# Three one-hots to a byte, and a deeper pipeline for the first spreading, in a two-layer graph kernel

## The chip, the cores and the metric

The kernel runs on one core of a Trainium2 chip. The metric is the device time in microseconds, the median of the runs. A separate profiled execution gives the trace that the text reads.

## The reference

There are 32768 nodes with 128 features and 524288 edges `src -> dst`, sorted by `dst`. Two layers follow one another:

- Layer 0 (cut): `agg = segment_sum(x[src], dst)`, then an MLP with batch norm on `(1 + eps) * x + agg`; attention with 8 heads inside blocks of 512 nodes; a second MLP; batch norms; and `x = layernorm(x + layer0(x))`.
- Layer 1 (cut), three times: `x = 0.5 * x + 0.5 * (softmax((x @ Wq.T + bq) @ keys.T) @ values - 0.2 * (x - dinv * scatter_add(dinv * x)))`. This is a memory lookup with 512 keys and a sum over the same edges in the other direction. Two layer norms end it.

So four times in all, rows are sent along the edges and summed at the other end.

## The kernel before, in words

Nodes are cut into 256 windows of 128 (`NW = 256`), or 64 blocks of four windows (`NB = 64`). Rows are kept as three bf16 parts (`ROW = 384` numbers), so that sums are exact enough. An exchange of rows along edges has two halves:

1. **Spreading** (`Exchange.spread`, L1444 to L1457). For each source window, a one-hot matrix of 128 lanes by 1536 slots (`SL = 2 * KS * P`) says which row goes to which slot. TensorE multiplies it with the window's rows, two blocks of 128 slots at a time, into a PSUM tile `exp` (L1449). VectorE or ScalarE turns each `exp` into bf16 in `y_o` (L1454). The two halves of `y_o` are stored into `slots` in HBM by the SP queue (L1457).
2. **Sums** (`Sums`, `Exchange.add`). For each destination window, `y_i` is loaded from `slots` (L1462), some rows are gathered by GpSimd (`listed`, L1471), VectorE makes a one-hot `oh` (L1482), and 19 matmuls per window add into `seg` (L1496).

The one-hot for spreading is called `pick`; it is 1 where a slot's listed lane equals the partition, and it is stored as fp8, in which 1.0 is the byte 0x38. In layer 0 each spreading makes its own `pick`. For layer 1, `keep_pick` (L1434) makes it once per window while layer 0's sums run, and stores it in HBM, 1536 bytes a partition (`pick_d`). The three spreadings of layer 1 load it again (`known_pick`, L1408, L1410), on the SP queue, two windows ahead (`ask_pick`, L2093).

The stages that the change touches, in order of time in the profile:

- `spread_x` (about 2330 to 3570 us): layer 0's spreading. Its order is written out by hand (`manual_schedule`). Window by window it loads x blocks (`load`, L1827), rows of the listing broadcast to all partitions (`row_of`, L1839, for odd windows; even ones use matmuls `row_p`, L1424), makes `pick` on VectorE (L1845, L1849), splits the rows (L1398 to L1400, L1396), and spreads. `sort_on` issues some of the sorting steps that a later stage needs after each pair of matmuls, so their number goes with the windows. `y_o`, `band` and `pick` have two buffers, `xe` three.
- `layer0_grid` (about 3570 to 5310 us): layer 0's sums, with part of the attention woven in; also written by hand. Per window, VectorE has the attention's maxima (L1642), the next window's `oh`, the `pick` for layer 1 (L1439, stored by L1441), and, when the window's sum has ended, its close (L1973, L1975; ScalarE's L1976 then frees the only `seg` buffer).
- the first loop of `layer1_grid` (about 5570 to 6770 us): the first spreading of layer 1, with layer 0's last norms. A scheduler sets the order from priorities (the numbers beside the steps). Every third eviction is VectorE's, the others ScalarE's.
- the second loop (about 6770 to 9010 and 9010 to 11180 us): sums of one step, the memory lookup, and the spreading of the next step, all woven together by the scheduler. Every fourth eviction is VectorE's.

The last stage (from 11180 us) has sums and the lookup only.

Of the kernel before, what the change touches and what calls it, by code (L numbers as in the profile page):

```python
# [9 lines left out]
F32 = mybir.dt.float32  # L10
I32 = mybir.dt.int32
# [9 lines left out]
P = 128  # L21
# [889 lines left out]
def tile_gnn_resnorm(ctx: ExitStack, tc: tile.TileContext, a: dict, out: bass.AP):  # L911
# [413 lines left out]
    rows_d = [dram(f"rows{t}", (N, ROW + 2 * (t == T_STEPS)), BF16) for t in range(T_STEPS + 1)]  # L1325
    pick_d = dram("pick", (NW, P, SL), FP8)
    gc = {}

    def grid_consts(pool):
        gc["iota1"] = pool.tile([P, P], BF16, name="iota1")  # L1330
        nc.vector.tensor_scalar(gc["iota1"], iota, 1.0, None, op0=OP.add)
        gc["lane1"] = pool.tile([P, 1], F32, name="lane1")
        nc.vector.tensor_scalar(gc["lane1"], lane_f, 1.0, None, op0=OP.add)
        gc["down"] = pool.tile([P, P], BF16, name="down")
        nc.vector.tensor_copy(gc["down"], gc["lane1"].to_broadcast([P, P]))
        gc["ident"] = pool.tile([P, P], BF16, name="ident_b")
        nc.vector.tensor_copy(gc["ident"], ident)
# [18 lines left out]
    class Exchange:  # L1356
# [8 lines left out]
        def __init__(self, key, slots, table):  # L1365
            self.grid, self.slots, self.table = grid.out[key], slots, table
            self.width = table.shape[1]
            self.bands = {}

        def load_rows(self, pool):  # L1370
# [37 lines left out]
        def known_pick(self, wp, w):  # L1408
            pick = wp.tile([P, SL], FP8, name="pick", bufs=3)
            nc.sync.dma_start(pick, pick_d[w])  # L1410
            return pick

# [21 lines left out]
        def keep_pick(self, wp, w, count):  # L1434

            def one():
                self.load_band(wp, w + 2)
                pick = wp.tile([P, SL], FP8, name="pick", bufs=2)
                nc.vector.tensor_scalar(pick, self.bands.pop(w), gc["lane1"], None, op0=OP.is_equal, op1=OP.add,  # L1439
                                        accum_out=count, saturate=False)  # L1440
                nc.sync.dma_start(pick_d[w], pick)  # L1441
            return [one]

        def spread(self, wp, pp, tag, w, pick, r, m, st, to_dve):  # L1444

            ps = pp.tile([P, 2, BLK], F32, name="exp", tag=tag)
            for j in range(2):
                o = (2 * m + j) * P
                nc.tensor.matmul(ps[:, j, :ROW], pick[:, o:o + P], r, start=True, stop=True)  # L1449
            if m == 0:  # L1450
                st["y"] = wp.tile([P, 2, KS, ROW], BF16, name="y_o")
            y = st["y"]
            dst = y.rearrange("p h r d -> p (h r) d")[:, 2 * m:2 * m + 2, :]
            (nc.vector.tensor_copy if to_dve else nc.scalar.copy)(dst, ps[:, :, :ROW])  # L1454
# [358 lines left out]
    def spread_x():  # L1813

        ex = Exchange("dst", slots_d[1], rows_d[T_STEPS])
        with tc.tile_pool(name="l0r", bufs=1) as gp, tc.tile_pool(name="l0e", bufs=2) as wp, \
                tc.tile_pool(name="l0e_p", bufs=2, space=PSUM) as p_k, \
                tc.tile_pool(name="l0e_e", bufs=3, space=PSUM) as p_e:
            grid_consts(gp)
            ex.load_rows(gp)  # L1820
            xb, rows, ends, picks, bands, y = {}, {}, {}, {}, {}, {}
            more = {"steps": grid.build_more(lane, Bank(p_k, "row_p")), "quota": 0.0}

            def load(b):
                if b < NB:
                    xb[b] = wp.tile([P, NCH, D], F32, name="xe", bufs=3)
                    nc.sync.dma_start(xb[b], rows_of(a["x"], b))  # L1827
# [6 lines left out]
            def row_of(w):  # L1834

                if w < NW:
                    bands[w] = wp.tile([P, SL], BF16, name="band")
                    src = ex.grid["row"][w % P:w % P + 1, w // P * SL:(w // P + 1) * SL]
                    nc.sync.dma_start(bands[w], src.to_broadcast([P, SL]))  # L1839
# [24 lines left out]
            with tc.manual_schedule():  # L1864
                load(0)
                load(1)
                split(0)
                for f in ends.pop(0):
                    f()
                row_of(1)  # L1870
                for j in range(SL // BLK):
                    pick(0, j)
                for w in range(NW):
                    b, c = divmod(w, NCH)
                    if w % 2:
                        row_of(w + 2)
                    if c == 0:
                        load(b + 2)
                        split(b + 1)
# [134 lines left out]
    def layer1_grid(v_d, s3, c3):  # L2014

        exs = [Exchange("src", slots_d[t % 2], rows_d[t]) for t in range(T_STEPS)]
        with tc.tile_pool(name="l1g", bufs=1) as gp:
            exs[0].load_tables(gp)
            for e in exs[1:]:
                e.slot, e.other, e.shared = exs[0].slot, exs[0].other, exs[0].shared  # L2020
            picked = {}

            def ask_pick(wp, w):
                if w < NW:
                    picked[w] = exs[0].known_pick(wp, w)

# [57 lines left out]
            def emit(t, b, st, wp, p_e, share):  # L2084
# [339 lines left out]
```

## Time and profile before

| | us |
|---|---|
| median of 5 runs (12862.94 to 12888.74) | 12870.88 |
| the profiled execution | 12879.18 |
| its span | 12877.0 |

| in the profiled execution | busy us | share |
|---|---|---|
| TensorE matmuls | 11136.2 | 86% |
| VectorE | 9300.9 | 72% |
| ScalarE | 6899.5 | 54% |
| GpSimd | 6111.3 | 47% |
| DMA, bytes moved | 3672.92 MB | mean 285 GB/s |

A share over the whole span mixes stages with different limits, so it says little by itself; the stages are read one by one below. A line such as "A <- B: 35.9, 42, 3.9" means that A waited for B 35.9 us in total, 42 times, at most 3.9 us. In a group of instructions, "x256" counts them, then follow the busy time, the mean time of one in ns, and the idle time of the engine just before them, with what ended it.

### The profile page before, as it was taken

What the parts mean: (1) busy time and instruction counts of PE and PEld (TensorE: products, weight loads), DVE (VectorE), ACT (ScalarE), POOL (GpSimd) and SP (SyncE); (2) the same over time, 40 slices, a digit from 0 to 9 for tenths busy, and PEclk for the clock granted to TensorE, in tenths of its full rate; (3) what the DMA queues carried; (4) which work ended last, traced back from release to release, by engine and by line L of the source; (5) the groups of instructions that cost most, each with busy time, mean ns of one, the idle gap of its engine ahead of it and who ended that gap; (6) DMA issues with size and microseconds to landing.
All of it is one profiled execution on the core that took longest, in us unless ns stands there. A gap on an engine that the chain in (4) does not pass through costs nothing.

```text
span 12877.0 us, 164812 instructions
## 1 busy us (share of the span) xinstructions
PE 11136.2 (86%) x57832; PEld 5540.5 (43%) x57832; DVE 9300.9 (72%) x14876; ACT 6899.5 (54%) x10523; POOL 6111.3 (47%) x5525
## 2 busy tenths in 40 slices
PE   7798798666679999966668999999999999899998
PEld 2233233332334444433324555555555555455554
DVE  7977977799778888666665666665566666587777
ACT  4455455677722333467775666666566666533333
POOL 0084075000067777200005666665666666577777
PEclk9899899899999999988889999999999999999999
DMA  1000000688899999779999999999999999988887
GB/s 44 10 15 20 10 14 14 239 327 325 325 320 334 334 338 343 262 287 342 345 344 336 400 397 396 393 393 375 377 398 398 395 395 391 361 293 290 287 289 254
DMA packets 1401340, 3672.92 MB, mean 285 GB/s; under 512 B 218802, under 2 KB 633682, under 8 KB 1399346
## 3 DMA queue, kind: packets, MB, share of 16 engines
q1 hardware_dynamic: 960496, 2952.44, 61.1%
q0 software_dynamic: 252608, 520.41, 12.5%
q10 hardware_dynamic: 187394, 189.42, 4.4%
q8 instruction: 457, 7.49, 0.2%
q14 instruction: 385, 3.15, 0.1%
HBM read 2175.76 MB, written 1485.80 MB: 284 GB/s over the span
## 4 chain that ended last, share of the span: by engine, by line
PE 43%; DMA 19%; DVE 18%; POOL 8%; ACT 7%; issue 4%; ACTq 0%; SPq 0%; DVEq 0%; POOLq 0%
PE seg L1496 14%; DMA slots<-y_o 12%; PE exp L1449 10%; ACT y_o L1454 5%; DVE y_o L1454 3%; PE s L2120 3%; POOL listed L1471 3%; PE s L1658 3%; DMA listed<-rows,other 3%; DVE mx L1642 3%; PE pv L1669 2%; PE tr L2126 2%; PE s L2132 1%; POOL moved L661 1%; POOL mask L662 1%
## 5 line engine op out<-in xcount | busy, mean ns | idle before, releaser
L1471 POOL DMA_INDIRECT listed<-rows,other x5120 | 5099.0, 996 | 4049.2 <-issue 2919.7
L1454 ACT CAST y_o<-exp 128x768 bf16<-128x768 f32 x4480 | 3380.4, 805 | 1229.7 <-PE exp L1449 759.3
L1449 PE MATMUL exp<-rows,pick 128*128 128x384 bf16 x10752 | 2558.6, 346 | 758.4 <-ACT y_o L1454 363.2
L1496 PEld LDWEIGHTS <-oh 128*128 128x128 bf16 x19456 | 1900.8, 98 | 1893.5 <-issue 803.6
L1496 PE MATMUL seg<-y_i,oh 128*128 128x384 bf16 x12288 | 2430.0, 327 | 17.9 <-DMA y_i<-slots 16.5
L1454 DVE CAST y_o<-exp 128x768 bf16<-128x768 f32 x1664 | 1587.3, 954 | 994.8 <-PE exp L1449 780.7
L1449 PEld LDWEIGHTS <-pick 128*128 128x128 fp8e4 x10752 | 1089.6, 102 | 2077.3 <-issue 1386.1
L1662 ACT ACTIVATE pT<-s 128x1024 f32<-128x1024 f32 x1024 | 1048.8, 1025 | 1174.9 <-PE s L1637 829.9
L1642 DVE TENSOR_REDUCE mx<-s 128x2 f32<-128x1024 f32 x1024 | 1246.0, 1220 | 283.0 <-PE s L1637 270.2
L1496 PE MATMUL seg<-listed,oh 128*128 128x384 bf16 (+1 forms) x5120 | 1208.2, 329 | 241.1 <-DMA listed<-rows,other 176.2
L1658 PE MATMUL s<-ql,k 32*128 32x512 f32 x4096 | 1225.1, 676 | 158.8 <-DVE mx L1642 146.2
L1637 PE MATMUL s<-k,q 32*128 32x512 f32 x4096 | 1232.7, 683 | 15.8 <-ACT pT L1662 10.8
L2196 DVE SCALAR_TENSOR_TENSOR part<-seg,dinv,part 128x128 f32<-128x128 f32 x1536 | 531.4, 346 | 946.7 <-PE seg L1496 935.0
L2120 PE MATMUL s<-keysT,qT 128*128 128x512 f32 x1536 | 812.5, 611 | 3.0 <-ACT pr L1064 1.8
L1482 DVE TENSOR_TENSOR oh<-iota,slot 128x2432 bf16<-128x2432 bf16 x512 | 725.0, 1416 | 4.2 <-DMA slots<-y_o 3.0
L1482 DVE TENSOR_TENSOR oh<-ramp_p,slot 128x2432 bf16<-128x2432 bf16 x512 | 722.3, 1411 | 3.4 <-DMA slots<-y_o 3.3
L1064 ACT ACTIVATE pr<-s,nm 128x512 f32<-128x512 f32 x768 | 533.4, 695 | 325.3 <-DVE nm L1062 324.0
L2132 PE MATMUL s<-pt,values 128*128 128x512 f32 x1536 | 699.5, 595 | 2.7 <-ACT pt L2127 2.7
L1658 PEld LDWEIGHTS s<-ql,k 32*128 32x128 f32 x4096 | 323.7, 193 | 691.2 <-DVE mx L1642 298.8
L1062 DVE TENSOR_REDUCE nm<-s 128x1 f32<-128x512 f32 x768 | 515.0, 681 | 121.9 <-PE s L2120 121.3
L1393 POOL MEMSET rows<- 128x8 bf16 x64 | 6.7, 106 | 1250.8 <-PE exp L1449 710.0
L1496 PE MATMUL seg<-common,oh 128*128 128x384 bf16 (+1 forms) x2048 | 586.8, 330 | 5.1 <-DMA common<-rows,shared 4.9
(409 smaller groups left out, 13930.6 us busy)
## 6 DMA issues: line engine op xcount, KB each, us to landing
slots<-y_o SPq DMA_DIRECT2D x2048, 576.0 KB
y_i<-slots SPq DMA_DIRECT2D x1024, 1152.0 KB
pick<-pick SPq DMA_DIRECT2D x1024, 192.0 KB
listed<-rows,other POOLq DMA_INDIRECT x5120
rows<-rows SPq DMA_DIRECT2D x192, 384.0 KB
band<-row_dst SPq DMA_DIRECT2D x128, 384.0 KB
band<-row_src ACTq DMA_DIRECT2D x256, 192.0 KB
x_d<-xn SPq DMA_DIRECT2D x128, 256.0 KB
```

What stands on the lines that cost most here:

```text
L1064: nc.scalar.activation(pr, s, AF.Exp, bias=nm, accum_out=sums)
L1449: nc.tensor.matmul(ps[:, j, :ROW], pick[:, o:o + P], r, start=True, stop=True)
L1454: (nc.vector.tensor_copy if to_dve else nc.scalar.copy)(dst, ps[:, :, :ROW])
L1471: nc.gpsimd.indirect_dma_start(out=g[:, k, :], out_offset=None, in_=self.table, in_offset=bass.IndirectOffsetOnAxis(ap=index[:, k:k + 1], ...
L1482: nc.vector.tensor_tensor(oh.rearrange("p c (w z) -> p c w z", z=2), ramp.rearrange("p (w z) -> p w z", z=2)[:, None].to_broadcast([P, NC2 ...
L1496: nc.tensor.matmul(ps[:, :n], oh[:, j, :], src, start=(k == 0), stop=(k == NC2 - 1))
L1637: nc.tensor.matmul(ps[:, s % 2, :], t["q", o][32 * s:32 * s + 32, c * P:(c + 1) * P], t["k", o][32 * s:32 * s + 32, :], start=True, stop=True)
L1642: nc.vector.tensor_reduce(m[:, c, 2 * i:2 * i + 2, xr[o]], st[b].pop(("two", i)), AX.X, OP.max, negate=True)
L1658: nc.tensor.matmul(ps[:, s % 2, :], t["k", o][32 * s:32 * s + 32, c * P:(c + 1) * P], t["ql", o][32 * s:32 * s + 32, :], start=True, stop= ...
L1662: nc.scalar.activation(t["p", c][:, 2 * i:2 * i + 2, :], ps, AF.Exp)
L2120: nc.tensor.matmul(s, st["q"][:, c * P:(c + 1) * P], keysT, start=True, stop=True)
L2132: nc.tensor.matmul(ps, values[:, k, :], st["pt"][:, k, :], start=(k == 0), stop=(k == NCH - 1))
```

## The change

There are two parts.

First, the `pick` kept for layer 1 is packed. Its 1536 bytes a partition are seen as 128x384 int32, in three thirds. A byte is 0x38 or 0, that is, bits 3, 4 and 5 are set together. `keep_pick` keeps bit 3 of the first third, bit 4 of the second and bit 5 of the last, in one 128x128 int32 tile (`three`), with one VectorE operation for the last third and one for each of the others, and stores that. A load is then 512 bytes a partition. `unpacked` makes the three thirds again with one VectorE operation (bitwise and with a mask by thirds). A set byte is then 0x08, 0x10 or 0x20, which in fp8 is 1/64, 1/32 or 1/8; the evictions multiply by 64, 32 or 8 (`WEIGHTS`), VectorE's with `tensor_scalar`, ScalarE's with `mul`. The load is asked two windows ahead as before, and unpacked one window ahead, after the third pair of matmuls of a window.

Second, in `spread_x`, `y_o` has five buffers (two elsewhere), `xe` four, `band` three; x blocks are loaded three blocks ahead, bands four windows ahead.

```diff
-    pick_d = dram("pick", (NW, P, SL), FP8)
+    pick_d = dram("pick", (NW, P, P), I32)
+    BITS = (3, 4, 5)
+    WEIGHTS = (64.0, 32.0, 8.0)
...
+        gc["bits"] = some[:, 1:].bitcast(I32)
+        for k in range(3):
+            nc.vector.memset(gc["bits"][:, k:k + 1].bitcast(U8), 1 << BITS[k])
...
         def known_pick(self, wp, w):
-            pick = wp.tile([P, SL], FP8, name="pick", bufs=3)
-            nc.sync.dma_start(pick, pick_d[w])
-            return pick
+            packed = wp.tile([P, P], I32, name="three", bufs=3)
+            nc.sync.dma_start(packed, pick_d[w])
+            return packed
+
+        def unpacked(self, wp, packed):
+            pick = wp.tile([P, 3, P], I32, name="pick")
+            nc.vector.tensor_tensor(pick, packed[:, None, :].to_broadcast([P, 3, P]),
+                                    gc["bits"].unsqueeze(2).to_broadcast([P, 3, P]), OP.bitwise_and)
+            return pick.rearrange("p k n -> p (k n)").bitcast(FP8)
...
                 nc.vector.tensor_scalar(pick, self.bands.pop(w), gc["lane1"], None, op0=OP.is_equal, op1=OP.add,
                                         accum_out=count, saturate=False)
-                nc.sync.dma_start(pick_d[w], pick)
+                packed = wp.tile([P, P], I32, name="three")
+                thirds = pick.bitcast(I32).rearrange("p (k n) -> p k n", k=3)
+                nc.vector.tensor_scalar(packed, thirds[:, 2], 0x01010101 << BITS[2], None, op0=OP.bitwise_and)
+                for k in (1, 0):
+                    nc.vector.scalar_tensor_tensor(packed, thirds[:, k], 0x01010101 << BITS[k], packed,
+                                                   op0=OP.bitwise_and, op1=OP.bitwise_or)
+                nc.sync.dma_start(pick_d[w], packed)
...
-                st["y"] = wp.tile([P, 2, KS, ROW], BF16, name="y_o")
+                st["y"] = wp.tile([P, 2, KS, ROW], BF16, name="y_o", bufs=self.kept)
...
-            (nc.vector.tensor_copy if to_dve else nc.scalar.copy)(dst, ps[:, :, :ROW])
+            if weight is None:
+                (nc.vector.tensor_copy if to_dve else nc.scalar.copy)(dst, ps[:, :, :ROW])
+            elif to_dve:
+                nc.vector.tensor_scalar(dst, ps[:, :, :ROW], weight, None, op0=OP.mult)
+            else:
+                nc.scalar.mul(dst, ps[:, :, :ROW], weight)
...
+            ex.kept = 5
...
-                    xb[b] = wp.tile([P, NCH, D], F32, name="xe", bufs=3)
+                    xb[b] = wp.tile([P, NCH, D], F32, name="xe", bufs=4)
...
-                    bands[w] = wp.tile([P, SL], BF16, name="band")
+                    bands[w] = wp.tile([P, SL], BF16, name="band", bufs=3)
...
-                        row_of(w + 2)
+                        row_of(w + 4)
                     if c == 0:
-                        load(b + 2)
+                        load(b + 3)
                         split(b + 1)
...
                     if m == 0:
                         ask_pick(wp, i + 2)
-                    ex.spread(wp, p_e, "exp", i, picked[i], st["r"][:, c, :], m, y, n % share == share - 1)
+                        if i not in picked:
+                            unpack(wp, i)
+                    ex.spread(wp, p_e, "exp", i, picked[i], st["r"][:, c, :], m, y, n % share == share - 1,
+                              WEIGHTS[m // 2])
+                    if m == 2:
+                        unpack(wp, i + 1)
```

More of the change, by code (lines that the diff above doesn't have):

```diff
@@ L1331, in grid_consts @@
         nc.vector.tensor_scalar(gc["iota1"], iota, 1.0, None, op0=OP.add)
-        gc["lane1"] = pool.tile([P, 1], F32, name="lane1")
+        some = pool.tile([P, 4], F32, name="lane1")
+        gc["lane1"] = some[:, 0:1]
         nc.vector.tensor_scalar(gc["lane1"], lane_f, 1.0, None, op0=OP.add)
@@ L1368, in __init__ @@
             self.bands = {}
+            self.kept = 2
         def load_rows(self, pool):
@@ L1440, in one, with spread @@
                                         accum_out=count, saturate=False)
-                nc.sync.dma_start(pick_d[w], pick)
+                packed = wp.tile([P, P], I32, name="three")
[5 more added lines that the diff above has]
+                nc.sync.dma_start(pick_d[w], packed)
             return [one]
-        def spread(self, wp, pp, tag, w, pick, r, m, st, to_dve):
+        def spread(self, wp, pp, tag, w, pick, r, m, st, to_dve, weight=None):
             ps = pp.tile([P, 2, BLK], F32, name="exp", tag=tag)
@@ L1864, in spread_x @@
             with tc.manual_schedule():
-                load(0)
-                load(1)
+                for b in range(3):
+                    load(b)
                 split(0)
@@ L1870, in spread_x @@
                 row_of(1)
+                row_of(3)
                 for j in range(SL // BLK):
@@ L2020, in layer1_grid, with unpack @@
                 e.slot, e.other, e.shared = exs[0].slot, exs[0].other, exs[0].shared
-            picked = {}
+            asked, picked = {}, {}
             def ask_pick(wp, w):
                 if w < NW:
-                    picked[w] = exs[0].known_pick(wp, w)
+                    asked[w] = exs[0].known_pick(wp, w)
+            def unpack(wp, w):
+                if w in asked:
+                    picked[w] = exs[0].unpacked(wp, asked.pop(w))
             def first(b, st, wp, p_tr, group):
```

## The prediction

> **What bounds the kernel now.** I began with the page's 40 slices, which show several regimes, and then asked for a table by stage. Columns: stage, its length, busy time of TensorE, its weight loads, VectorE, ScalarE and GpSimd, then granted clock, DMA share, GB/s.
>
> ```profile
> core 0: us, PE busy (x) PEld busy (x) DVE busy (x) ACT busy (x) POOL busy (x), PEclk, DMA share, GB/s
> ...
> 2330.00:3570.00 1240.00, 824.17 (x3716) 373.30 (x3716) 1083.98 (x1481) 927.02 (x1318) 12.43 (x70) 0.94 0.88 321
> 3570.00:5310.00 1740.00, 1606.21 (x9263) 787.16 (x9263) 1450.27 (x2046) 499.57 (x861) 1240.35 (x1312) 0.97 0.97 332
> ...
> 5570.00:6770.00 1200.00, 768.38 (x3174) 353.50 (x3175) 772.97 (x1524) 845.37 (x1176) 0.00 (x0) 0.83 0.94 341
> 6770.00:9010.00 2240.00, 2114.87 (x10825) 1178.62 (x10825) 1339.30 (x2153) 1399.20 (x2314) 1369.20 (x1324) 0.99 1.01 385
> 9010.00:11180.00 2170.00, 2056.11 (x10579) 1143.94 (x10577) 1303.82 (x2102) 1351.52 (x2225) 1345.25 (x1301) 1.00 1.02 390
> ```
>
> I call these five S (first spreading), L0 (first layer's sums), P (first spreading of layer 1), W1 and W2 (sums and spreading together). The change touches no other stage. W1 and W2 have a full DMA system (share above 1) and TensorE at 94%. In L0 TensorE, VectorE (83%) and DMA are all near full. P is slack on each engine by itself, so there the handovers bind. S has VectorE at 87%.
>
> Next come the waits inside stages. In S, then in P (who waits for whom, total us, times, longest):
>
> ```profile
> ACT y_o L1454 <- DMA slots<-y_o: 123.6, 105, 3.9
> ...
> DVE pick_b L1845 <- DMA band<-row_dst: 35.9, 42, 3.9
> ```
> ```profile
> DVE y_o L1454 <- PE exp L1449: 322.2, 337, 1.5
> ...
> PE exp L1449 <- DVE y_o L1454: 256.9, 244, 2.4
> ```
>
> In steady L0 (4500 to 5100 us, 91 windows of 6.59 us each) the largest VectorE wait is the one below: it waits for a window's sum to end.
>
> ```profile
> DVE hn L1973 <- PE seg L1496: 39.3, 48, 3.7
> ```
>
> In steady W2 (9300 to 11100 us, 217 one-hots L1482, so 8.29 us a window) TensorE's waits before the spreading are short:
>
> ```profile
> L1449 PE MATMUL exp<-rows,pick 128*128 128x384 bf16 x2595 | 596.8, 324 | 56.0 <-ACT y_o L1454 46.4 <-DVE y_o L1454 1.4 <-DMA pick<-pick 0.7
> ```
>
> **Prices.** VectorE's integer and small groups in the first stage, then three groups of the page (busy, mean ns of one, idle before):
>
> ```profile
> L743 DVE TENSOR_TENSOR moved<-moved,mask 128x768 int32<-128x768 int32 x2 | 1.9, 958 | 0.1
> ...
> L728 DVE TENSOR_SCALAR moved<-moved 128x768 int32<-128x768 int32 x2 | 1.1, 552 | 0.0
> L510 DVE SCALAR_TENSOR_TENSOR sh_a<-keys,word 128x128 f32<-128x128 f32 x2 | 0.6, 292 | 0.1
> ...
> L705 DVE COPY keys<-word 128x128 f32<-128x128 f32 x2 | 0.4, 216 | 0.0
> ```
> ```profile
> L1454 ACT CAST y_o<-exp 128x768 bf16<-128x768 f32 x4480 | 3380.4, 805 | 1229.7 <-PE exp L1449 759.3
> ...
> L1662 ACT ACTIVATE pT<-s 128x1024 f32<-128x1024 f32 x1024 | 1048.8, 1025 | 1174.9 <-PE s L1637 829.9
> ```
>
> - *Unpack*, 128x384 int32, two tensors: L743's 768 take 958 ns and L221's 1024 take 1217, so 1.01 ns an element and 181 fixed: 570 ns by that line, 552 if 128 elements are taken off L2077 (128x512, also with a broadcast operand, 682 ns). I take 0.55 us; 256 in P, W1 and W2 each: 141 us of VectorE a pass.
> - *Pack*, three on 128x128 int32: 216 (L705, one source) + 2 x 285 (just under L510) = 0.79 us a window, 202 us in L0.
> - *ScalarE's scaled eviction* becomes an ACTIVATE: L1662 less 256 elements at 0.86 ns (from L2108's 512 at 584 ns to L1454's 768 at 805) is 804 ns, so nothing. With a pointer operand it would cost 0.1 us more (L2114, 688 for 512, against L2108), 106 us in 1024 a pass; the instruction list names none, so I take 0.
> - *VectorE's scaled eviction*: between 954 (the CAST) and 1012 (L1849's 745 for 512, which has a pointer, plus 256 elements). 0 to 25 us a pass; I take 10.
> - *Loads and stores*: the one-hot goes from 128 packets of 1536 B to 128 of 512 B. The DMA queues between 1500 and 2300 us (almost only 512 B packets on q10), then between 9100 and 11100 us (packets, MB, share of 16 engines):
>
> ```profile
> q10 hardware_dynamic: 8448, 4.20, 1.8%
> ```
> ```profile
> q1 hardware_dynamic: 186094, 652.25, 83.2%
> ```
>
> The first is 1.8% x 800 us x 16 / 8448 = 27 ns for 497 B; the second 143 ns for 3505 B. The line through both gives 67 ns for 1536 B and 28 ns for 512 B. With 8 packets an engine, one load falls from 0.54 to 0.22 us: 0.32 us a window, 81 us of full DMA time in each of L0, P, W1, W2.
>
> A rule speaks against this: the Trainium skill's "DMA: Bandwidth & Descriptors", section Bandwidth, measures 0.95 us for 64 KB and says transfers below that size are descriptor-dominated. By that figure, an estimate, the small load costs 0.73 us more than my row says, and with 0.54 us before it the 81 us saved would become 105 us lost a pass. [...]
>
> **Part by part.**
>
> *S.* Five y_o buffers in place of two, band and x loads further ahead. This removes ScalarE's 124 us of waits for stores and VectorE's 36 for bands (and 13 for stores), but what is late next? From 2400 to 3200 us VectorE is busy 47.2 of each 50 us, because sorting steps are paced by windows and go along with them; that part can shrink by 5.6%, 45 us, and I take 25. From 3200 to 3560 the waits for stores and bands are 34 and 19 us and VectorE has room; I take 25 of the 53. The queue order changes little: the loads move ahead on SP, whose waits there are for evictions. S: -50, between -110 (most of the waits) and +10 (a deeper queue at share 0.88 lengthens each transfer).
>
> *L0.* VectorE's busy time a window is 519.9/91 = 5.71 us, with 0.88 idle. Pack makes it 6.50 of 6.59. Queued behind it are the close of the sum (L1973, L1975), for which ScalarE's L1976 and then TensorE wait (one seg buffer). The 0.43 us a window of waiting for seg can be absorbed; the other 0.45 (uT, bands, aval, handovers) cannot be counted on: 6.50 + 0.45 = 6.95, +0.36 x 256 = +92. The relieved queue gives back part of the stage's waits for bands (39 us on VectorE) and gathered rows (29 us on TensorE): -25. On SP the pick store L1441 now waits for pack, and the y_i load behind it leaves 0.8 us later, covered by its two windows' lead. L0: +67, between -30 (TensorE had all the slack) and +200.
>
> *P.* 141 us more on a VectorE with 427 us idle. The unpack stands between evictions; TensorE already waits 257 us for VectorE's evictions. In the instruction order two of four unpacks of a block fall between plain evictions, where VectorE idles about 1 us each time, and two beside the split or the moments, where they add up. I take a quarter: +35, and 3 for scaled evictions. P: +38, between -20 (the DMA share of 0.94 falls) and +141.
>
> *W1, W2.* The DMA floor falls from 8.29 to 7.97 us a window. TensorE is busy 96% of steady time, 7.97 us too. So both allow at most 81 us a pass; TensorE's waits for y_o and y_i (56 + 5 us in 1800, 75 in 2200) should fall and not vanish. VectorE rises from 61 to 68%, and its evictions are what TensorE hardly waits for (1.4 us). I take 57 a pass, -115 for both; between -162 and +30 (no relief, and a tenth of 282 us of unpacking exposed).
>
> Sum: -50 + 67 + 38 - 115 = -60. The profiled execution took 12879.2 us (span 12877.0), 8 above the median of the five runs, 12870.9. On the median: **12811**.
>
> **Rivals.** *A, slower: VectorE's new work is exposed.* Place: pack before the close in L0, unpack before the evictions in P. Full price 202 + 141 = 343 us, against 190 us of relief (50 + 25 + 115): +153, 13024. It decides from 55% exposed; I have 38% (130 of 343). For: VectorE at 99% in L0 leaves no play, and the profile has 257 us of TensorE behind VectorE in P. Against: half of L0's windows end with VectorE waiting.
> *B, nothing: TensorE holds W1 and W2.* Its 96% is all it needs and half the gain is left, -57: total about -2, 12869. For: the full TensorE. Against: its busy time is modelled, with matmuls in isolated pairs (0.49 us) that would close up.
> *C, faster: DMA time is the limit wherever the share is near 1.* W1 and W2 give 162, S 85, L0 all its 81 against the 92, P nothing: -162 - 85 + 11 = -236, 12635. For: shares of 0.97 to 1.02. Against: L0's VectorE.
> That the one-hot is not smaller in HBM can't be: the stored tensor is 128x128 int32.
>
> **How the numbers follow.** Forecast 0.47, A 0.23, B 0.15, C 0.15. About 0.2% (26 us) is what this kernel's measurement can tell from no change. Faster: forecast 0.44, C 0.15, B 0.03: 0.62. Same: forecast 0.03, B 0.10: 0.13. Slower: A 0.23, B 0.02: 0.25. The range 12680 to 12965 leaves out the far half of A and of C; the forecast's own is 12740 to 12850.
>
> **What would show it.** Right: W1 and W2 near 8.05 us a window with DMA still above 0.97; L0 near 6.85 us with VectorE above 93%; waits of y_o for slots gone from S; the unpack near 550 ns, the three packing operations near 0.79 us together. Wrong: W1 or W2 no shorter (B); L0 over 1900 us or TensorE's wait for VectorE's y_o in P above 350 us (A); the 512 B loads' packets over 50 ns (then the relief is under a half).

## The result, and the profile after

The changed kernel takes **12873.93 us** (median of 25 runs, 12851.41 to 12902.96) beside 12872.83 for the kernel before (46 runs): a ratio of 1.0001, 95% interval 0.9996 to 1.0007. I had forecast 12811, and 0.62 for a gain that can be measured. No difference can be measured. The profiled execution of after has a span of 12866.5 us, 10.5 below that of before.

Six of the ten kernels whose ratios are given below, and four of those that ran once, ran where the kernel before takes 14.09 ms and not 12.87, with L0 some 370 to 470, W1 and W2 290 to 530 and the last stage 340 to 440 us longer than the same code has elsewhere, and with the attention, S and P as ever; each ratio is to the kernel before in the same runs, and W1 and W2 are compared within one of the two groups only.

The table by stage of after, with the columns of the one before (S, L0, P, W1, W2):

```profile
core 0: us, PE busy (x) PEld busy (x) DVE busy (x) ACT busy (x) POOL busy (x), PEclk, DMA share, GB/s
2347.00:3527.00 1180.00, 822.45 (x3721) 367.29 (x3719) 1071.30 (x1495) 926.92 (x1318) 12.26 (x68) 0.94 0.92 338
3527.00:5340.00 1813.00, 1622.27 (x9260) 791.16 (x9260) 1644.19 (x2806) 494.34 (x860) 1242.17 (x1312) 0.98 0.93 299
...
5600.00:6850.00 1250.00, 770.17 (x3168) 362.78 (x3169) 879.09 (x1766) 851.91 (x1175) 0.00 (x0) 0.83 0.82 302
6850.00:9010.00 2160.00, 2072.89 (x10715) 1167.38 (x10715) 1447.51 (x2397) 1382.93 (x2271) 1391.00 (x1312) 0.99 1.00 379
9010.00:11167.00 2157.00, 2067.14 (x10696) 1157.87 (x10694) 1440.25 (x2385) 1387.34 (x2269) 1379.04 (x1312) 1.00 1.01 381
```

S is shorter. VectorE has some 195 us more in L0 and the stage is longer. P has lost DMA share (0.94 to 0.82) and not time. W1 and W2 are shorter at a DMA share that is still 1.

The borders of the stages can be read more closely from the first and last start of an instruction that stands at each (first eviction into `y_o`, the copies of `slot`, the last copy into `degs`, the first `oh` of W1, the last eviction). All stages in this text are read so. "Only part 2" (e1_again) and the control (c1_changed, the changed kernel again) were timed beside the same runs of the kernel before:

| us | S | L0 | P | W1 + W2 | attention, before S | between L0 and P | last |
|---|---|---|---|---|---|---|---|
| before | 1245.3 | 1726.7 | 1247.8 | 4352.5 | 2340.0 | 265.0 | 1699.7 |
| after | 1187.4 | 1805.1 | 1299.0 | 4259.3 | 2347.1 | 268.7 | 1699.9 |
| change | -57.9 | +78.4 | +51.2 | -93.2 | +7.1 | +3.7 | +0.2 |
| only part 2 | 1186.5 | 1716.9 | 1257.6 | 4345.5 | 2346.5 | 271.3 | 1699.4 |
| control | 1190.9 | 1806.4 | 1301.9 | 4269.4 | 2347.7 | 271.3 | 1703.3 |
| forecast change | -50 | +67 | +38 | -115 | 0 | 0 | 0 |

All four terms have the forecast's sign, and their sum is -21 us, or -10 with the small changes of the other stages. Where they come from, view by view. In S, the waits for stores (124 us on ScalarE before) and bands (36) are 2 and 4 us; what is left is the handover between TensorE and ScalarE, and the wait for the matmul `row_p`:

```profile
PE exp L1470 <- ACT y_o L1476: 187.7, 505, 1.0
...
DVE pick L1876 <- PE row_p L1439: 79.8, 55, 3.8
```

In steady L0 VectorE is busy 556 of 600 us (520 before), and a window takes 6.98 us in place of 6.59 (86 windows against 91):

```profile
4500.00:5100.00 600.00, 550.81 (x3193) 267.58 (x3192) 556.08 (x950) 172.64 (x298) 417.46 (x442) 0.99 0.93 303
```

In P, TensorE's wait for VectorE's evictions has become smaller (257 to 209 us), and a new one stands beside it, for the unpack itself (who waits for whom, total us, times, longest):

```profile
PE exp L1470 <- DVE y_o L1478: 208.5, 226, 1.4
...
PEld L1470 <- DVE pick L1424: 104.4, 55, 2.2
...
PE exp L1470 <- DVE pick L1424: 80.7, 54, 1.5
```

In steady W2 (9300 to 11100 us; 223 windows of 8.07 us) TensorE's group, as before, and two waits. The first of the waits, the unpack's for its load, is new, and no line of my forecast has it:

```profile
L1470 PE MATMUL exp<-rows,pick 128*128 128x384 bf16 x2663 | 625.0, 325 | 25.1 <-ACT y_o L1480 19.3 <-DVE y_o L1478 1.0
```
```profile
DVE pick L1424 <- DMA three<-pick: 143.6, 96, 4.8
ACT y_o L1480 <- DMA slots<-y_o: 65.8, 55, 4.4
```

The prices, from the groups of VectorE and ScalarE (busy, mean ns, idle before):

```profile
L1478 DVE TENSOR_SCALAR y_o<-exp 128x768 bf16<-128x768 f32 x1280 | 1219.4, 953 | 625.4 <-PE exp L1470 553.8 <-DMA slots<-y_o 33.5 <-ACT y_o L1480 17.4
L1424 DVE TENSOR_TENSOR pick<-three,lane 128x384 int32<-128x384 int32 x768 | 424.0, 552 | 317.5 <-DMA three<-pick 311.6 <-PE s L2169 3.0 <-PE exp L1470 2.4
...
L1460 DVE SCALAR_TENSOR_TENSOR three<-pick,three 128x128 int32<-128x128 int32 x512 | 149.9, 293 | 17.5
L1458 DVE TENSOR_SCALAR three<-pick 128x128 int32<-128x128 int32 x256 | 64.2, 251 | 8.9
```
```profile
L1480 ACT ACTIVATE y_o<-exp 128x768 bf16<-128x768 f32 x3328 | 2572.9, 811 | 993.0 <-PE exp L1470 704.3 <-DMA slots<-y_o 171.3 <-issue 45.3
```

The unpack at 552 ns is as forecast, the pack at 251 + 2 x 293 = 837 ns (0.79 us forecast), ScalarE's scaled eviction at 811 (804), VectorE's at 953 (954 to 1012; I had taken 10 us a pass for it, of which only 3 in P went into the sum, and there is nothing).

### The profile page after: what moved, and what is told of

The parts are those of the page before. It is cut to its first block, busy times and chain, and to the rows that moved or that the text cites. A ratio compares the mean times of both kernels' runs of the same rounds, so it can differ in the third digit from the quotient of the medians.

```text
span 12866.5 us, 165746 instructions
## 1 busy us (share of the span) xinstructions
PE 11111.3 (86%) x57832; PEld 5544.6 (43%) x57832; DVE 9835.9 (76%) x16418; ACT 6920.7 (54%) x10523; POOL 6168.8 (48%) x5525
## 4 chain that ended last, share of the span: by engine, by line
PE 30%; DMA 9%; DVE 6%; POOL 3%; ACT 3%; issue 3%; SPq 0%; DVEq 0%; ACTq 0%; POOLq 0%
PE seg L1522 10%; PE exp L1470 10%; DMA slots<-y_o 5%; DMA listed<-rows,other 4%; POOL listed L1497 3%; PE s L2169 3%; PE s L2157 3%; DVE y_o L1478 3%; ACT y_o L1480 2%; PE tr L2163 2%; PE s L2149 1%; ACT pr L1064 1%; DMA three<-pick 1%; DVE pick L1424 1%; PE tr L2143 0%
## 5 line engine op out<-in xcount | busy, mean ns | idle before, releaser
L1480 ACT ACTIVATE y_o<-exp 128x768 bf16<-128x768 f32 x3328 | 2572.9, 811 | 993.0 <-PE exp L1470 704.3
L1522 PE MATMUL seg<-y_i,oh 128*128 128x384 bf16 x12288 | 2504.3, 328 | 4.4 <-DMA y_i<-slots 4.3
L1478 DVE TENSOR_SCALAR y_o<-exp 128x768 bf16<-128x768 f32 x1280 | 1219.4, 953 | 625.4 <-PE exp L1470 553.8
L1688 ACT ACTIVATE pT<-s 128x1024 f32<-128x1024 f32 x1024 | 1047.8, 1024 | 1134.0 <-PE s L1663 817.4
L1668 DVE TENSOR_REDUCE mx<-s 128x2 f32<-128x1024 f32 x1024 | 1245.3, 1220 | 271.0 <-PE s L1663 267.9
L1476 ACT CAST y_o<-exp 128x768 bf16<-128x768 f32 x1152 | 856.9, 809 | 241.7 <-PE exp L1470 169.6
L1424 DVE TENSOR_TENSOR pick<-three,lane 128x384 int32<-128x384 int32 x768 | 424.0, 552 | 317.5 <-DMA three<-pick 311.6
```

Source lines behind the costliest of these rows:

```text
L1478: nc.vector.tensor_scalar(dst, ps[:, :, :ROW], weight, None, op0=OP.mult)
L1480: nc.scalar.mul(dst, ps[:, :, :ROW], weight)
L1522: nc.tensor.matmul(ps[:, :n], oh[:, j, :], src, start=(k == 0), stop=(k == NC2 - 1))
L1668: nc.vector.tensor_reduce(m[:, c, 2 * i:2 * i + 2, xr[o]], st[b].pop(("two", i)), AX.X, OP.max, negate=True)
L1688: nc.scalar.activation(t["p", c][:, 2 * i:2 * i + 2, :], ps, AF.Exp)
```

## The experiments

My theory after the result: the terms are real, stage by stage, and cancel; S gains without the packing, and the packing by itself is a loss. The rivals are named with each run. "The changed kernel" is the one after. e4, e5, e6 and e10 to e14 ran once each, so their stages are those of one profile and have no interval.

### One part at a time: e1, e2, and e1 again with a control

e1 is the kernel before with only the second part of the change (`y_o` 5, `xe` 4, `band` 3 buffers, loads further ahead); e2 is the changed kernel with that part undone; c1 is the changed kernel.

> Only the second part: the first spreading with five y_o, four xe and three band buffers and loads asked further ahead; the one-hots stay 1536 B a partition, as before. Theory 1 (the terms add up, and each stage's time is its own): S is 58 us shorter, as in the changed kernel, and no other stage moves: 12815 us, ratio 0.9955. Rival (S gains only together with the packing, or what it gains is given back by the sorting steps and the stage after it): 12860 to 12875 us, ratio 0.999 to 1.000.

> Only the first part: one-hots packed in L0 and unpacked in P, W1 and W2; the first spreading as before. Theory 1 (L0 +78, P +51, W1 and W2 -93 each add up, +36, and some 10 us elsewhere): 12905 to 12920 us, ratio 1.003 to 1.004, so the packing by itself is slower. Rival (the packing is neutral and the second part gives nothing): 12870 us, ratio 1.000.

Measured where before takes 14092 us: e1 0.9962 (0.9947 to 0.9978), e2 1.0087 (1.0070 to 1.0104). S is 1184.9 us in e1 and 1245.8 in e2, P is 1250.6 and 1300.3: both as forecast there. Both verdicts fall as theory 1 has it, but e2's by other terms: beside e1, its L0 is no longer (2177 us against 2179) and its W1 and W2 are 91 us longer (4802 against 4711), where I had +78 and -93. So e2 does not show theory 1's terms; the next two runs do.

> The changed kernel itself, as a control beside the others of this call. The runs e1 to e7 had a time before of 14092 us, with L0 near 2180 us, W1 and W2 above 4550 us and the last stage near 2090 us in every one of their profiles, while S, P and the attention stage took what they took in the first two profiles. Theory 1 (these long stages come of the surroundings of those runs, not of the kernels): with a time before near 12870, L0 is 1805 us, W1 and W2 4259 us, ratio 1.000; with a time before near 14092, the terms of S, L0 and P still hold, and the ratio is e2's less S's 58 us, 1.005. Rival: the changed kernel itself reacts to those surroundings, and the ratio there is above 1.010.

> Only the second part, the same kernel as in e1. Theory 1: S is 58 us shorter and nothing else moves: 12815 us, ratio 0.9955 (e1 had 0.9962). Rival: what S gains is given back later: ratio 0.999 or more.

Where before takes 12874.63: e1 12807.76, ratio **0.9956** (0.9943 to 0.9970); c1 12876.40, ratio 1.0006 (0.9997 to 1.0015), with L0 at 1806 us: the long L0 of e2 is not the kernel's. So the second part is worth -67 us by the medians, or -57 by the ratio (-39 to -73 by its interval), and S has 58 of it in the profile; the first part, which is what lies between the two, costs 12876.40 - 12807.76 = **+69 us** (+64 by the two ratios). The two profiles of the table say where: L0 +89, P +44, W1 and W2 -76, S and the last stage +4 each, about 0 in the other two: +67 of spans. The attention's 7 us and the 4 us between L0 and P, which the first two profiles showed, are scatter of single profiles: over all kernels here they lie between 2332 and 2353, and 265 and 271.

### L0 and the bytes: e5 and e6

e5 takes the pack away and keeps the small store; e6 keeps all work of VectorE and ScalarE and moves all the bytes of before.

```diff
 e5
-                packed = wp.tile([P, P], I32, name="three")
...
+                packed = pick.bitcast(I32).rearrange("p (k n) -> p k n", k=3)[:, 2]
 e6
-    pick_d = dram("pick", (NW, P, P), I32)
+    pick_d = dram("pick", (NW, P, 3, P), I32)
...
-            packed = wp.tile([P, P], I32, name="three", bufs=3)
+            packed = wp.tile([P, 3, P], I32, name="three", bufs=3)
...
-                nc.sync.dma_start(pick_d[w], packed)
+                nc.sync.dma_start(pick_d[w], thirds)
```

> The changed kernel with L0's three packing operations left out: L0 stores the last third of the one-hot as it is, so two thirds of layer 1's one-hots are left out of the computation. Theory 1 (L0 had VectorE as its bound, and the smaller store gave back little): L0 at 1690 to 1720 us, the packing's price 85 to 115 us of its 207 us of VectorE time. Rival (the queue was L0's other bound, and its relief is as large as I priced it, up to 81 us): L0 at 1640 to 1680 us, and the packing alone costs 125 us or more. Other stages as in the changed kernel.

> The changed kernel with all its work on VectorE and ScalarE, but the packed one-hot lies in a third of a tensor of 1536 B a partition, and stores and loads move all of it, as before the change. Theory 1 (W1 and W2 are shorter because of the DMA bytes alone, and VectorE's new work there is hidden): W1 and W2 back at 4340 to 4360 us; P at 1300 to 1350 us; L0 at 1805 to 1840 us. Rival (VectorE's new work costs W1 and W2 part of the relief): W1 and W2 at 4370 to 4420 us.

L0 of the control, of e5 and of e6 (columns as above):

```profile
3539.00:5345.00 1806.00, 1618.04 (x9260) 789.96 (x9260) 1642.24 (x2799) 494.70 (x860) 1241.80 (x1312) 0.98 0.92 300
```
```profile
3537.00:5249.00 1712.00, 1602.74 (x9260) 785.74 (x9260) 1446.90 (x2031) 497.74 (x860) 1240.42 (x1312) 0.98 0.95 316
```
```profile
3526.00:5333.00 1807.00, 1623.27 (x9260) 791.14 (x9260) 1642.73 (x2800) 494.89 (x860) 1241.51 (x1312) 0.98 0.95 318
```

With the pack, L0 takes 1806 to 1807 us whether the store has 512 or 1536 B a partition; without it 1712, where e1, with neither pack nor small store, has 1717. So the pack costs 94 us of its 195 us on VectorE, and the smaller store brings about 5 (1717 less 1712, within the scatter of single profiles), though the DMA share was 0.97 before. L0's order is written out by hand, so no other order of instructions comes in. The gross +92 of my forecast was right; the 25 us that I took off for the relieved queue do not exist.

W1 and W2 are 4353.9 us in e6, against 4269.4 in the control and 4352.5 before: VectorE's 282 us of unpacking there are hidden, and the gain comes with the smaller loads, or with the order in which the scheduler then lays TensorE's instructions (on this see e11 to e14). In steady W2 (9300 to 11100 us), the queue that carries them, before and after:

```profile
q1 hardware_dynamic: 167579, 587.37, 83.4%
```
```profile
q1 hardware_dynamic: 171764, 572.85, 82.0%
```

83.4% of 1800 us over 217 windows is 6.92 us, 82.0% over 223 is 6.62: the queue's own time fell by 0.30 us a window, close to the 0.32 that I worked out from the two packet lengths. The window itself fell by less: over 216 windows of each pass, from the start of one `oh` to that of another, it has 8.31 to 8.35 us before and in e1, and 8.13 to 8.17 after and in the control, which is 0.15 to 0.20 us of the 0.30.

Against the small load I had set the Trainium skill's "DMA: Bandwidth & Descriptors", section Bandwidth, with 0.95 us for 64 KB. My estimate of a loss put that beside 0.54 us of my own for the large load; the page's own table has larger times for larger transfers, so by itself it says no such thing. Here the stages with the small loads are 85 us shorter over the two passes (e6 against the control). The page's table was measured with transfers issued from GpSimd, these loads are issued on SP's queue, and no run here times one load by itself.

### The new wait of the unpack: e3, e3 again

The packed load is asked two windows ahead, but unpacked one window ahead, so it has some 1.3 windows to land. e3 gives it one more.

```diff
-            packed = wp.tile([P, P], I32, name="three", bufs=3)
+            packed = wp.tile([P, P], I32, name="three", bufs=4)
...
-                        ask_pick(wp, i + 2)
+                        ask_pick(wp, i + 3)
```

> The changed kernel with the packed load asked three windows ahead in four buffers (two windows in three buffers before), so that the unpack, which comes more than half a window before its window, has 2.3 windows of lead in place of 1.3. Theory 1: VectorE's waits for the packed load (312 us, 208 times) fall below 60 us and carry a part of the relief that W1 and W2 did not give (93 in place of 115 us): both together 20 to 40 us shorter than in the changed kernel, 12835 to 12855 us, ratio 0.997 to 0.9985. Rival (TensorE is full in W1 and W2 and the wait is covered): the waits vanish from the list and the time stays, 12868 to 12880 us, ratio 1.000.

> The changed kernel with the packed load asked three windows ahead, in four buffers; the same kernel as in e3. Theory 1 (the unpack's wait for its load costs TensorE time): W1 and W2 at 4220 to 4240 us where the changed kernel has 4259; ratio to the changed kernel 0.997 to 0.9985; where the time before is near 14092 it is e3's 0.989 again. Rival (the wait is covered, since TensorE was 98.5% busy): W1 and W2 within 10 us of the changed kernel's, and the same time where the time before is near 12870; what e3 gained then belongs to its surroundings alone.

e3: 0.9889 (0.9867 to 0.9912), W1 and W2 4551 us; e3 again: 1.0003 (0.9994 to 1.0012), 4266 us, the control's 4269. In the second the rival holds: the wait for `three` is gone from the list of steady W2, and ScalarE's wait for stores, which was 66 us, has taken its place:

```profile
ACT y_o L1480 <- DMA slots<-y_o: 133.2, 63, 6.2
```

So the new wait was no part of the missing relief: it is gone, the time stays, and a wait for stores on the same queue has grown in its place. Why e3 gained where before takes 14092 us is open.

### P, and what the unpack costs there: e4, e10, e12

e4 spreads layer 1 with one fixed one-hot and drops the unpack; e10 drops the loads too; e12 keeps loads and unpacks, but TensorE reads the fixed tile.

```diff
-                    picked[w] = exs[0].unpacked(wp, asked.pop(w))
+                    picked[w] = fixed[id(wp)]          # e4; e10: no load either
...
+                    exs[0].unpacked(wp, asked.pop(w))  # e12
+                    picked[w] = fixed[id(wp)]
```

> The changed kernel with the unpack left out: the packed loads run as in the changed kernel, but layer 1 spreads with one fixed one-hot tile, so what layer 1 sends along the edges is left out of the computation. Theory 1 (P pays for the unpack itself, W1 and W2 hide it): P falls from 1299 by the 51 us it had gained and by the queue's relief too, to 1210 to 1250 us; W1 and W2 stay at 4240 to 4270 us. Rival (a part of the unpack is exposed in W1 and W2 too): W1 and W2 at 4150 to 4200 us.

> As e4_no_unpack, and the loads of the one-hots in P, W1 and W2 are left out too. Theory 1 (the DMA queues are what holds W1 and W2): a 512 B load is worth about 0.2 us of DMA time a window, so W1 and W2 lose a further 80 to 110 us, to about 4150 us. Rival (TensorE, 98.5% busy, holds them): less than 30 us more than e4_no_unpack. P is below e4_no_unpack by 0 to 50 us.

> The changed kernel with all its loads and unpacks, but TensorE spreads with one fixed tile (what layer 1 sends is left out of the computation), so that nothing waits for the unpack. Its groups of spreading matmuls have 2.38 on average. Theory 1 (order): bytes and VectorE's work are the changed kernel's, and W1 and W2 are 4310 to 4340 us, as in e4. Rival (bytes and VectorE's work decide): 4255 to 4275 us, the changed kernel's. P: the unpack still takes VectorE's time but TensorE doesn't wait for it: between 1250 and 1300 us, and where it lies says how much of P's 50 us is VectorE's time and how much the wait.

| us | P | W1 + W2 | where before takes |
|---|---|---|---|
| control | 1301.9 | 4269.4 | 12.87 ms |
| e6, loads of 1536 B, unpack | 1302.1 | 4353.9 | 12.87 |
| e4, loads of 512 B, no unpack | 1249.3 | 4332.1 | 12.87 |
| e10, no loads, no unpack | 1136.6 | 4395.4 | 12.87 |
| e12, loads of 512 B, unpack not waited for | 1248.2 | 4761.0 | 14.09 |

P first. Without the unpack it is 1249 us, and with the unpack on VectorE, but nobody waiting for it, 1248: there, its 141 us of VectorE time cost nothing. The 50 us go with TensorE's wait for its result, the two new lines of P above; the wait isn't parted from the order of VectorE's instructions in P, some hundreds of which the scheduler also laid otherwise in e12. The bytes don't matter (1302 with either load), yet without any load P falls by another 113 us. That was not in my picture of P at all, and led to e16.

W1 and W2 went against both my theories: less work, longer time (three profiles of the changed kernel's W1 and W2, after, the control and e5, lie between 4259 and 4275, so 63 and 126 us are more than scatter). With each edit the scheduler lays TensorE's instructions otherwise. Counting the spreading matmuls that stand together between the sums' gives 3.03 a group before, 2.98 in e6, 2.55 after, 2.35 in e4 and 2.28 in e10 (over all of W1 and W2 in the traces, with the long groups at their ends, 3.13, 3.08, 2.64, 2.44 and 2.34). In e10 the queues are no less busy, only less fast (before: 1.03 and 395 GB/s in the same stretch):

```profile
9300.00:11100.00 1800.00, 1684.46 (x8837) 965.61 (x8835) 1079.20 (x1758) 1147.93 (x1857) 1088.69 (x1079) 0.99 1.00 366
```

So a DMA share of 1 is not the floor that I took it for. e10 has the share with 7% fewer bytes a second.

### The same order, three sizes of load: e11, e13, e14

With the loads on ScalarE's queue the scheduler gives 2.28 for either size, and e11 has the same without loads; the matmuls of these three stand in nearly the same order: the traces, with 57831 matmuls each, differ in 52 to 148 lines.

```diff
-            nc.sync.dma_start(packed, pick_d[w])
+            nc.scalar.dma_start(packed, pick_d[w])      # e13 (on e6), e14 (on the changed kernel)
...
+            return self.bands[id(wp)]                   # e11: one fixed tile, no load
```

> The changed kernel without the packed loads: VectorE unpacks one fixed tile for every window, so what layer 1 sends is left out of the computation; all other work is the changed kernel's. In e4_no_unpack and e10_no_loads W1 and W2 became longer with less work (4332 and 4395 us, against 4266), and with each the scheduler laid TensorE's spreading matmuls in smaller groups between the sums: 2.55 a group in the changed kernel (3.03 before), 2.35 in e4, 2.28 in e10. This kernel's order has 2.28 too and is e10's but for a hundred lines. Theory 1 (the order sets W1 and W2, more than bytes or VectorE): 4380 to 4410 us. Rival (e10 was longer because the unpack was missing, and the loads' bytes are what holds W1 and W2): 4150 to 4220 us.

> e6_wide (all the changed kernel's work, with 1536 B stores and loads) with the loads asked on ScalarE's queue in place of SP's. The scheduler then lays TensorE's spreading in groups of 2.28, the same order as e11's and e14's but for some tens of lines. Theory 1 (order): 4380 to 4420 us whatever the bytes. Rival (bytes): more than e14 by the 89 us that lay between e6 and the changed kernel.

> The changed kernel with its 512 B loads asked on ScalarE's queue: the order of e11 and e13, the bytes of the changed kernel. Theory 1 (order): W1 and W2 4380 to 4410 us, within 20 us of e11 and e13, and the whole about 120 us longer than the changed kernel. Rival (bytes): 80 to 95 us less than e13, 40 us more than e11.

All three ran where before takes 14087 us, so my numbers for theory 1 can't be compared, but the three can with each other. W1 and W2: e11 4568.8, e14 4611.4, e13 4665.2. At one order, 512 B a partition go with 43 us and the other 1024 B with a further 54: the rival's direction, and less than the 85 by which e6 and the control differ. But kernels with the same W1 and W2 lie up to 62 us apart in such runs (e2 4801.6, e17 4739.5), so the three profiles don't prove that the bytes count. What of the 85 is the order's, which differs between e6 and the control, stays open. How much order alone is worth stays open too: the order of 2.28 had 4395 us without loads where the changed kernel has 4269, and 4611 where e2 and e7, with the changed kernel's W1 and W2, have 4802 and 4749.

P in these three: 1163, 1212 (e14) and 1171 us (e13), all with the full unpack, all below the 1248 of before.

### Packing somewhere else: e7, e8

e7 stores the plain one-hot in L0; P spreads with it as before and packs there for W1 and W2. e8 adds e3's change.

```diff
+    wide_d = dram("wide", (NW, P, SL), FP8)
...
+                nc.sync.dma_start(wide_d[w], pick)          # L0, in place of the pack
...
-                    if m == 2:
-                        unpack(wp, i + 1)
+                    if m == 2 and not t:
+                        ex.pack(wp, i, picked[i])           # P: the three operations and the store
+                    elif m == 2:
+                        unpack(wp, i + 1)
```

> The changed kernel with the packing moved: L0 stores the one-hot unpacked as before; P loads it unpacked, spreads with it as before (no unpack, no scaling), and there packs it for W1 and W2 on VectorE, where no engine waits for the packed tile before W1. Theory 1 (L0's price is VectorE's pack in a stage that VectorE fills, and P's price is TensorE's wait for the unpack): L0 back to 1727 us; P at 1253 to 1310, since the three packing operations (0.81 us a window) stand between evictions but nothing waits for their result; W1 and W2 as in the changed kernel, 93 us shorter than before: 12745 to 12800 us, ratio 0.990 to 0.995. Rival (P is bound by VectorE's and the queue's total work, now 0.81 us a window in place of 0.55 and 21 MB more stores): P above 1340 us, 12810 to 12850 us.

> e7 with the packed load asked three windows ahead in W1 and W2, in four buffers: L0 and P as in e7 (no packing in L0; P loads 1536 B one-hots, packs on VectorE and neither unpacks nor scales). Theory 1 (the terms add up): S -58, L0 0, P +90 (1338 in e7's profile), W1 and W2 -93 to -130, some +10 elsewhere: 12780 to 12820 us, ratio 0.993 to 0.996, the best so far. Rival (in P and L0 the costs only change places): 12840 us or more.

e7: 1.0049 (1.0033 to 1.0064) where before takes 14092, with P at 1338.5: theory 1 had 1253 to 1310 and missed, and the rival's 1340 is near. e8: 12817.38 us, **0.9959** (0.9946 to 0.9973), with L0 1717.4, P 1336.8, W1 and W2 4266.2. L0's 89 us came back, and P took 79 of them (1257.6 in e1): here the pack stands between VectorE's evictions, and TensorE waits for those (257 us before):

```profile
PE exp L1479 <- DVE y_o L1485: 326.7, 251, 2.6
```

e8's 0.9959 lies within the interval of e1, which packs nothing. The relief of W1 and W2 (79 us against e1) pays for the pack in P, and no more.

### The place of P's loads: e16, e17

```diff
-                        ask_pick(wp, i + 2)
+                        ask_pick(wp, i + 2, nc.sync if t else nc.scalar)
```

> e1 (only the second part, one-hots of 1536 B a partition, no packing) with the loads of P, and only these, asked on ScalarE's queue in place of SP's, where they stand between the stores of y_o. In e13 and e14 (all loads on ScalarE's queue) P took 1171 and 1212 us, with all of the unpacking in it, against 1302 and 1299 us with the loads on SP's. Theory 1 (P's time hangs on when the one-hot's load is issued, more than on VectorE): P falls from 1250 to 1257 us to 1130 to 1180 us and no other stage moves; beside e1's 12808 us that is 12680 to 12740 us, ratio 0.986 to 0.990 (where the time before is near 14090, by the same microseconds: 0.987 to 0.991). Rival (without the unpack, TensorE never waited for P's loads, so their queue is of no account): P at 1245 us or more, 12800 us, ratio 0.9955.

> The changed kernel with the loads of P, and only these, asked on ScalarE's queue. Theory 1: P falls from 1299 to 1200 to 1220 us, as in e14, below the 1248 us of before although VectorE unpacks in it; all other stages as in the changed kernel: 12780 to 12795 us, ratio 0.992 to 0.994 (0.998 to 1.000 where the time before is near 14090). Rival (P's 51 us are VectorE's time for the unpack): P at 1285 us or more, ratio 0.999 to 1.001.

Before takes 14087 us here. e17: 0.9962 (0.9947 to 0.9978), P 1205.2 us. e16: **0.9886** (0.9865 to 0.9906), 13917 us, P 1135.6. In both, P is where theory 1 put it; e17's ratio is lower than the 0.998 to 1.000 that I gave, for which I have no cause. In the changed kernel's P TensorE waits for the unpack; in e17's that wait isn't among the first lines any more, and TensorE's granted clock is up (0.83 in P before and after). That the clock alone makes P shorter is unlikely: in e3 again it is 0.77 in P, and P takes 1297 us, as the control does at 0.83 (1302). P of e17, then of e16:

```profile
6000.00:7190.00 1190.00, 780.63 (x3324) 356.43 (x3322) 890.94 (x1802) 878.88 (x1230) 0.00 (x0) 0.88 0.90 330
```
```profile
6000.00:7130.00 1130.00, 757.80 (x3328) 349.32 (x3328) 786.59 (x1553) 880.16 (x1232) 0.00 (x0) 0.90 1.00 379
```

e16's P equals e10's, which has no loads at all (1136.6): with this edit, 192 KB a window cost nothing in P. How it acts is open. On SP each load stands between stores that wait for evictions (SP's own waits for VectorE's `y_o` were 579 us between 5700 and 6700 before, 597 after), so I thought that a load asked two windows ahead leaves late. But in P no engine's wait is put down to a load of `pick`, neither before nor in e1. The wait that fell is TensorE's for VectorE's evictions, 257 us before and 256 in e1; in e16, from 6000 to 7132 us:

```profile
PE exp L1450 <- DVE y_o L1455: 83.6, 163, 1.9
```

The scheduler also laid VectorE's instructions in P otherwise: e16's trace differs from e1's in 342 lines of some 1550, and e17's from the control's in 766 of some 1800 (TensorE's matmuls in 10 and 12). VectorE's order is thus a rival to the queue itself, and no run parts the two; it stands against e10's 113 us in the same way.

e16 has the lowest ratio of those tried: no packing, deeper buffers in S, and one queue changed in P. Beside e1's 0.9962 in the same surroundings, this last edit is worth 0.9886 / 0.9962 = 0.9924. It was not timed where before takes 12.87 ms, and e3's 0.9889 came to 1.0003 there. Unlike e3's, though, e16's gain lies in P (1250.6 us in e1, 1135.6 in e16), which e1 has at 1257.6 where before takes 12.87 ms.

## Why the prediction was wrong, by its own steps

- *The sum.* I had -50 for the second part and 67 + 38 - 115 = -10 for the first. The runs show -67 and +69 by the medians. The first part's net is what failed: each of its three terms was too kind, by 22, 6 and 39 us (+89, +44 and -76 in the profiles of e1 and the control); S and the last stage, at +4 each, and the scatter of profiles make the rest of the 79.
- *S, -50.* -58 in S and -57 to -67 in all. Right, and alone it would have been a faster kernel.
- *L0, +67.* +78 to +89. The gross +92 is what the pack costs (94); the mis-sized term is the -25 for a relieved queue, which measured about -5. The waits for bands and gathered rows, from which I took it, were real, but a third of the store's bytes does not shorten the stage (e6).
- *P, +38.* +44 to +51. Near in size, wrong in kind: a quarter of VectorE's time exposed was not it. VectorE's time costs nothing where no engine waits for the unpack (e12); the 50 us come and go with TensorE's wait for it (e4, e12). I had listed the unpack among VectorE's evictions, and not asked who waits for the unpack itself. That the number came near is luck.
- *W1 and W2, -115.* -76 to -93. The queue's saving was right (0.30 of 0.32 us a window); what was too large is the share of it that the time follows: I took 57 of 81 us a pass, and it was 38 to 47, or 0.15 to 0.20 us of 0.30 a window. Why no more follows is open; TensorE's other order is one candidate. That VectorE's unpacking costs nothing there was right (e6). The load's wait, which I had not listed, costs nothing (e3 again).
- *The rivals.* B, "nothing", named the result, and 12869 is near, but its mechanism gave W1 and W2 -57, with +67 and +38 as forecast; they gave more and the others cost more, so its number is right by luck. A's mechanism, exposed work on VectorE, holds in L0 to 48% (94 of 195 us); with P's 50 of 141 it is 43% in all, under its 55%. C's, that time follows DMA wherever the share is near 1, fails in L0, where the bytes bring about 5 of 81 us, and W1 and W2 gave about half of its 162.
- *The chances.* I gave 0.62 to a gain on the strength of a net of 60 us. The first part's three terms were too kind by 68 us together; the chances left too little room for errors that all lie on one side.

## What to carry to other kernels

When a change trades a full engine's time in one stage for bytes in another, put the parts apart and time each: here one was -57 to -67 and the other +64 to +69, and a total of nothing hid a gain that the second part alone keeps. A DMA share near 1 doesn't say what fewer bytes are worth: at 0.97 the smaller store brought L0 about 5 us of 81, and at 1.0 W1 and W2 gave about half of what the queue saved. And when a load is put before a new operation, ask who waits for that operation. Where a scheduler sets the order, compare the orders too: asking P's loads on another queue, which also moved VectorE's instructions, was worth more than all that was done to make them small.

## What the runs showed of the hardware that I had not expected

- A DMA share of 1 does not mean a full rate: with a share of 1.00 to 1.03, steady W2 moved 395 GB/s before, 389 after and 366 in e10, and a window took longest where the fewest bytes were moved (8.44 us in e10, 8.32 before, 8.13 after).
- In L0 a third of the store's bytes changed nothing (1806 and 1807 us) at a DMA share of 0.92 and 0.95.
- The scaled eviction of 128x768 out of PSUM costs VectorE what the plain one does (953 ns against 948 in S), and ScalarE too (811 against 809).
